# Another written order of 48 interleaved strands, with 13 unread products in place of 52

## The chip, the cores and the metric

The kernel runs on one core of one Trainium2 chip. The metric is device time in microseconds (us) of one execution; the figure of a version is the median of its runs.

## What is computed

The reference is two layers over x of shape (4, 512, 128), float32. Each layer normalises x, runs an attention s and a mixture of experts g on the result, and adds their gated product:

```python
xn = _layernorm(x)
s = _L0_attn_ref(xn, ...)            # three branches: compressed, selected, window of 32
g = _silu(_L0_ffn_ref(xn, ...))      # 8 experts, 2 of them per token
x = x + s * g
xn = _layernorm(x)
s = _L1_attn_ref(xn, ...)            # full attention, 16 heads of 8, plus residual
g = _silu(_L1_ffn_ref(xn, ...))      # one of 8 experts per token is kept
x = x + s * g
```

An expert is a 128 to 512 to 128 network with relu. Layer 1's batches are the 4 batches of 512 tokens again; its attention takes all 512 keys of a batch.

## The kernel before, in words

The work is cut into 48 generators, called strands. Each `yield` ends a step: a handful of instructions, mostly on one engine. Nothing in the program decides at run time which strand goes next. A string, `ORDER`, names the strand of every step, and `advance` walks through it and issues the step's instructions. The five engines (PE is TensorE, DVE VectorE, ACT ScalarE, POOL GpSimd, SP the queue of most transfers) each get their instructions in that order, and the framework adds the semaphore waits and leaves the order alone (`manual_schedule`). So the string sets the order of every queue.

```python
        self.advance(dict(zip(string.digits + string.ascii_letters, strands)))
...
        for s in "".join(ORDER.split()):
            if s == ".":
                self.busy()
            else:
                next(strands[s], None)
```

A `.` calls `busy` (L1247): one 128x128 product of the identity with itself into a part of a PSUM tile that nobody reads. It leaves two matmul records in the trace.

The characters stand for these strands, in the order of the list in `both`; in the text a letter with a number is the n-th step of a strand:

- 0 to 3: layer 0's norm, transpose, router and gate logits of one batch each; 4 to 7: `enter`, the end of layer 0 and the start of layer 1 for one batch. Its steps: 1 loads the picked expert rows (`yg`, on SP), 2 to 4 weigh and add them (POOL, DVE, DVE), 5 tanh on ACT, 6 silu, gate with `s` and add x (DVE), 7 to 10 layer norm (DVE, POOL, DVE, POOL; step 10 is six POOL instructions), 11 and 12 transpose and copy, 13 and 14 router logits, 15 to 18 queries (product, split into high and low parts, four writes to DRAM, one strip read of 1 MB), 19 to 22 the same for keys, 23 and 24 values.
- 8, 9: small set-up of layer 0 and of layer 1 (`lnb`). a, b: routing of batches 0, 1 and of 2, 3 (`route`, with `dispatch`): step 2 the rank product, 3 to 5 DVE, 6 the product that inverts the list, 7 the lists of rows and experts.
- c to f: values of layer 0's attention per batch; g to j: keys and queries; k to n: the attention itself (steps 1 and 4 window scores, 7 compressed scores, 10 selected scores, 13, 14, 16, 17 the weighted sums `o` of one tile each, 15 and 18 their normalisation on DVE, 19 to 22 transpose, copy, output projection, addition).
- o, p, q, r: layer 0's experts in 46 tiles of 128 rows. o loads a tile's weights (578 KB, SP), p fetches its rows (indirect, POOL), q transposes four tiles' rows, then per tile the hidden product `hid` (L367) and relu to `h` (ACT), r the output product `y` (L394), the bias addition on DVE (L403) and the scattered store to `ys` (POOL, L406). Weight buffers: four; `hid` and layer 0's `y` have one PSUM buffer each, so a y product needs the addition of the one before it.
- s: buffers of layer 1's values. t, u: layer 1's scores, top-2 and the scaled rows `xw` stored to `xs` (t of batches 0, 1; steps 5 and 7 are the stores). v: layer 1's routing over all tokens.
- w, x: layer 1's attention in 64 units: w the scores `st` (L1079) and two exponentials of 1021 ns on ACT, x the weighted sum `av` (L1100). y, z, A, B: turning and projecting its result per batch.
- C, D, E, F: layer 1's experts, 23 tiles, like o, p, q, r but with relu on DVE. G: silu of layer 1's expert rows, step 1 loads them. H to K: last gate and store per batch. L: the certificate.

Some couplings set by the order: strand E needs v's lists, v needs all four batches' router logits, and so `enter` of batches 2 and 3, which needs all of r and the attention of batch 3 (n22). The scores of unit after unit reuse two PSUM pairs that ACT must have read. The k strip of a batch (step 22 of `enter`) is loaded into the buffer that held attention probabilities of layer 0.

Of the kernel before, what the change touches and what calls it, by code (L numbers as in the profile page):

```python
# [62 lines left out]


ORDER = """
v800010....00.c1201c2c31102319283139c12a2323a2a8.gaa8.........aaaoapoaa8aopgo.............3pg3bp
pp.....bggpb..qpqpqqrpbqpqrboqrqgrprbbbqorqr8bcqrbgcorrcgcpbrqb...cgorgpkcppkqkggg...kqrkrkqgork
qrkrqkorqkrkrqqkorrrqpgoqdgrdhdphhphhqpqhrrqdqrrrqoqrroqqrqphoqqhrqrdprdqdorrdqdprhhpqokrdqrrkor
rkkrqqorrrqpkoqrqkpqrpqqrphhkhoqkrqrqqqrpqkhohrrkhpriorriipreipoeireiiiliiqe.iiill......lqrilirl
orijeejjeleelelljflfjlfljjjlfjjq.jjllqrjlffqfffrlqorrlrfjjorlljlmqm4qqrp5qrqmpoqmrprmprqmorqm44r  # L70
m45qmr5or4m54qrmqrq4orr5qm4pqmr4or5qpqr5pqqrpmorrm4mr4oq4qmr555rmqqqq4qrq4orrrqpqomrrmpqqrmpom4r
r4pq4rqrrqosq5rn5orrnp4rqnppppppppoq5rr5ttrqtqorrqq4qqqtqnttttr4ror4nrqnrrqonrorrnqnrqnorrnqnq5r
ooooorr5q5rqrrqqnrrqqr5rqqqrrrnrrnnnss4675n455..w66wn46w776.w7wx6w6w7wx6w6665n6wwx6w6ww6w6xw6xw5
wx5wwxwyynwnwx7ww7wxwx777ww7x7w7w7wxuwyywuuwxwwwxwvwxwvxwywwxwwv66wwvx6wwx6uwxwuuwxyuuvvwyCwywxC
ywyCywCDwx6D6w6wDwxDwx7Dw7wx7DwyDwyzwEDzwxDwEwEEDwxDwwEEDwxwxwFzwFECzFExwwxwFwFECwFEwExDEwxDwwxD
FzFwCDzwEEFwxwwxwFwFECwFE7wxwwxwx7z7wwx7zzzwzFzFCFzwwEEwxwwxw77w7wxwxFwFACwFAEwEEExDwxDwwDFwFECD
wEwxFwwxwxFwFACwFAEwExwwxwFwFECwFEwxwwxwxFEFECFEEAwDAwxDwFEDDDDDDDDFECwFwxwFwFECwFEwxwwxwxFEFECF
AwALwxwFEwEwExEAwFACFwAwxwAAwwxwxFEFECFwwxwFEFECFwwxwFwFECwFEwxwwxwxBFBwFwECEFEwxEwwxwBBFEFECCCC
CFwwxwFEFEFwwxwxFEFEEFwwxwBFBwFwxFwFwFwxFFwwxxxBGBLLBBLBBGBGGHHHGGGGGIIIJJJKKK
"""  # L80


# [2227 lines left out]
```

## Time and profile before

| | before |
|---|---|
| median of 3 runs | 508.03 us (505.74 to 514.65) |
| profiled execution | 502.39 us |
| its span, first to last instruction | 500.6 us |
| mean granted TensorE clock | 0.939 |
| matmuls | 4355 records, busy 432.1 us |

The times of steps and waits come from the profiled execution, so a sum of them is compared with its 502.39 us and 500.6 us. The page gives busy time per engine, the chain that ended last and the costliest groups of instructions; the trace answers for stretches of time, waits and single instructions. In its rows a bracket at the end says how long the engine stood idle before the instruction and what it waited for. DMA-issuing rows (SPq, POOLq) are issues: the data lands later.

### The profile page before, as it was taken

The page shows a single profiled execution, that of the slowest core. Times are in us where ns is not written, and L with a number is a line of the kernel's source. Part 1 is how long each engine was busy: PE and PEld are TensorE (multiplying, and loading weights), DVE is VectorE, ACT ScalarE, POOL GpSimd, SP SyncE. Part 2 cuts the span into 40 slices and gives each one's busy share as a digit, 9 for nine tenths or more (in the row PEclk, how much of TensorE's full clock was granted, in tenths as well). Part 3 has the DMA queues.
Part 4 walks back from the last instruction along what each step waited for, and adds up shares of the span by engine and source line. Part 5 has one row for each costly group of instructions (what it writes and reads, how often), then busy time and mean ns, then how long its engine had stood idle before and what let it go on. Part 6 is the DMA issues. An engine that isn't in the chain of part 4 may idle for free.

```text
span 500.6 us, 11299 instructions
## 1 busy us (share of the span) xinstructions
PE 432.1 (86%) x4355; PEld 307.7 (61%) x4355; DVE 270.6 (54%) x819; ACT 246.2 (49%) x417; POOL 176.8 (35%) x194
## 2 busy tenths in 40 slices
PE   5977799798999898989598969789899999999950
PEld 5765687787768787978477723224454556656620
DVE  5797754156767728444432666695235434643445
ACT  1101773543384375234262157667567676667530
POOL 2136535534500166976032250404441144121300
PEclk9997999999999899979799579999899999999985
DMA  8834546955665366359975632039547744544233
GB/s 269 199 107 145 164 130 205 248 174 175 202 138 108 106 197 185 119 173 255 316 227 181 206 132 85 0 122 313 198 125 229 231 134 119 163 125 139 64 97 89
DMA packets 50302, 82.49 MB, mean 165 GB/s; under 512 B 5520, under 2 KB 30240, under 8 KB 50240
## 3 DMA queue, kind: packets, MB, share of 16 engines
q1 hardware_dynamic: 45248, 71.30, 46.9%
q0 software_dynamic: 4416, 9.05, 7.2%
q10 hardware_dynamic: 576, 1.34, 0.7%
q8 instruction: 36, 0.59, 0.5%
q14 instruction: 26, 0.21, 0.1%
HBM read 64.56 MB, written 17.11 MB: 163 GB/s over the span
## 4 chain that ended last, share of the span: by engine, by line
PE 44%; DVE 14%; DMA 6%; issue 4%; POOL 4%; ACT 2%; SPq 0%; ACTq 0%; POOLq 0%; DVEq 0%
PE av L1100 10%; PE y L394 8%; PE hid L367 6%; PE st L1079 4%; DMA wt<-in_w 2%; PE o L838 2%; PE sw L761 2%; PE otr L1118 1%; DMA xr<-xs,d_where 1%; PE so L891 1%; PE o L830 1%; POOL xr L344 1%; DVE yg L437 1%; ACT h L379 1%; DVE yg L432 1%
## 5 line engine op out<-in xcount | busy, mean ns | idle before, releaser
L1088 ACT ACTIVATE p<-st 128x1024 f32<-128x1024 f32 x128 | 124.2, 1021 | 75.3 <-PE st L1079 75.2
L406 POOL DMA_INDIRECT ys<-y,d_where x69 | 69.3, 1005 | 181.4 <-DVE y L403 123.9
L344 POOL DMA_INDIRECT xr<-xs,d_where x69 | 67.5, 978 | 78.6 <-DMA xs<-xw 24.4
L394 PEld LDWEIGHTS y<-wt,h 128*128 128x128 f32 x552 | 70.8, 196 | 36.8 <-ACT h L379 15.8
L394 PE MATMUL y<-wt,h 128*128 128x128 f32 x552 | 81.9, 293 | 10.7 <-ACT h L379 6.3
L367 PE MATMUL hid<-xts,wt 128*128 128x128 f32 x552 | 79.9, 290 | 10.5 <-DMA wt<-in_w 6.4
L379 ACT ACTIVATE h<-hid,wt 128x128 f32<-128x128 f32 x184 | 52.4, 369 | 73.2 <-issue 40.7
L367 PEld LDWEIGHTS hid<-xts,wt 128*128 128x128 f32 x552 | 70.9, 201 | 17.6 <-issue 7.2
L1100 PE MATMUL av<-p,va 128*32 128x512 f32 x512 | 70.0, 619 | 1.3 <-ACT p L1088 1.1
L403 DVE TENSOR_TENSOR y<-y,wt 128x128 f32<-128x128 f32 x69 | 19.9, 289 | 93.0 <-PE y L394 73.2
L1079 PE MATMUL st<-stq,stk 32*128 32x512 f32 x256 | 40.7, 507 | 5.2 <-ACT p L1088 5.1
L381 DVE TENSOR_SCALAR h<-hid,wt 128x128 f32<-128x128 f32 x92 | 25.9, 343 | 24.9 <-PE hid L367 24.9
L1079 PEld LDWEIGHTS st<-stq,stk 32*128 32x128 f32 x256 | 16.6, 186 | 36.0 <-ACT p L1088 27.1
L770 ACT ACTIVATE pw<-sw 128x1024 f32<-128x1024 f32 x16 | 15.6, 1021 | 14.0 <-PE sw L761 14.0
L1100 PEld LDWEIGHTS av<-p,va 128*32 128x32 f32 x512 | 10.2, 108 | 16.8 <-issue 12.4
L1110 DVE COPY oT<-av 128x512 f32<-128x512 f32 x16 | 11.0, 688 | 15.1 <-PE av L1100 15.1
L362 ACT COPY xts<-xt 128x512 f32<-128x512 f32 (+2 forms) x18 | 10.3, 572 | 17.6 <-PE xt L359 17.6
L838 PE MATMUL o<-v,pc 128*128 128x36 f32 x128 | 18.4, 292 | 0.0
L838 PEld LDWEIGHTS o<-v,pc 128*128 128x128 f32 x128 | 16.5, 201 | 0.8
L761 PEld LDWEIGHTS sw<-qT,kw 32*128 32x128 f32 x512 | 16.4, 194 | 0.5 <-issue 0.3
L761 PE MATMUL sw<-qT,kw 32*128 32x64 f32 x512 | 16.3, 275 | 0.0
L359 PE MATMUL xt<-c_ident,xr 128*128 128x128 f32 x69 | 12.1, 287 | 4.4 <-DMA xr<-xs,d_where 4.0
(254 smaller groups left out, 597.5 us busy)
## 6 DMA issues: line engine op xcount, KB each, us to landing
wt<-in_w SPq DMA_DIRECT2D x69, 578.0 KB, 4.0
v<-drv SPq DMA_DIRECT2D x16, 256.0 KB, 6.2
drq<-hl SPq DMA_DIRECT2D x16, 256.0 KB, 3.3
stq<-drq SPq DMA_DIRECT2D x4, 1024.0 KB, 5.2
drk<-hl SPq DMA_DIRECT2D x16, 256.0 KB, 3.0
stk<-drk SPq DMA_DIRECT2D x4, 1024.0 KB
yg<-ys SPq DMA_DIRECT2D x12, 256.0 KB, 3.1
xr<-xs,d_where POOLq DMA_INDIRECT x69, 4.4
```

Source lines behind the costliest of these rows:

```text
L344: nc.gpsimd.indirect_dma_start(out=rows[i // 4][:, i % 4, :], out_offset=None, in_=self.xs[ks[i // NS]], in_offset=bass.IndirectOffsetOnAx ...
L367: nc.tensor.matmul(ps[:, f, :], wt[:, W_1 + f * P : W_1 + (f + 1) * P], xt[:, i % 4 * P : (i % 4 + 1) * P], start=True, stop=True,)
L379: nc.scalar.activation(h[:, f, :], ps[:, f, :], AF.Relu, bias=b1)
L381: nc.vector.tensor_scalar(h[:, f, :], ps[:, f, :], b1, 0.0, ALU.add, ALU.max)
L394: nc.tensor.matmul(ps[:, 0:D], g["h"][:, f, :], g["w"][:, W_2 + f * D : W_2 + (f + 1) * D], start=(f == 0), stop=(f == NF - 1),)
L403: nc.vector.tensor_tensor(y, ps[:, 0:D], g["w"][:, W_B2 : W_B2 + D], ALU.add)
L406: nc.gpsimd.indirect_dma_start(out=views[i], out_offset=bass.IndirectOffsetOnAxis(ap=to[:, i % NS : i % NS + 1], axis=0), in_=y, in_offset ...
L761: nc.tensor.matmul(ps[g // 2][:, g % 2, jj * 2 * QB : (jj + 1) * 2 * QB], a["kw"][g32(g), j].rearrange("p h r -> p (h r)"), qT[g32(g), j * ...
L838: nc.tensor.matmul(out(0, g, 4), pc[g // 2][:, g % 2, t * P : (t + 1) * P], flat(a["vc"][:, g]), start=True, stop=True,)
L1079: nc.tensor.matmul(ps[hp][:, i, :], ks[r, t, k * P : (k + 1) * P], qs[r, t, :], start=True, stop=True,)
L1088: nc.scalar.activation(e, ps[hp], AF.Exp, scale=SCALE)
L1100: nc.tensor.matmul(av[32 * h : 32 * h + 32, :], va[:, k, (4 * t + h) * 32 : (4 * t + h) * 32 + 32], e[h // 2][:, h % 2, :], start=(k == 0) ...
```

## The change

Only the string `ORDER` is replaced. It has 1287 steps in place of 1326, because it has 13 dots in place of 52. All other strands have as many steps as before, in their own order, so the instructions of the computation, their shapes and their buffers are the same; what changes is how the strands lie against each other on all five queues.

- The dots between the routing of batches 0, 1 and the first experts (positions 48 to 109) go from 30 to 7; those further on go from 17 to 1. The first five stay.
- Set-up strand 8 ends at step 34 of the string, not at 140. Values and keys of batch 0 (c, g) and its attention (k) come earlier: c ends at 88 (was 169), k starts at 121 (was 168).
- Attention of batch 3 (n) ends at 685, just after the first scores of layer 1 (w1 at 679); before, it ended at 779, after w22 (w1 at 720).
- The loads of `enter` 2 and 3 (6, 7) come after the first units of layer 1's attention; `u` and `v` (scores and routing of layer 1) lie closer together, the stores u5 and u7 now ahead of v2. Layer 1's experts start at 849 (was 901).
- At the end the load G1 stands before the last scores' sums (x78), not behind them, and the gates of batches 0 and 1 (H1, I1) before the last addition of s (B13), not behind it.

```diff
--- before.py
+++ after.py
@@ -63,20 +63,20 @@
 
 
 ORDER = """
-v800010....00.c1201c2c31102319283139c12a2323a2a8.gaa8.........aaaoapoaa8aopgo.............3pg3bp
-pp.....bggpb..qpqpqqrpbqpqrboqrqgrprbbbqorqr8bcqrbgcorrcgcpbrqb...cgorgpkcppkqkggg...kqrkrkqgork
-qrkrqkorqkrkrqqkorrrqpgoqdgrdhdphhphhqpqhrrqdqrrrqoqrroqqrqphoqqhrqrdprdqdorrdqdprhhpqokrdqrrkor
-rkkrqqorrrqpkoqrqkpqrpqqrphhkhoqkrqrqqqrpqkhohrrkhpriorriipreipoeireiiiliiqe.iiill......lqrilirl
-orijeejjeleelelljflfjlfljjjlfjjq.jjllqrjlffqfffrlqorrlrfjjorlljlmqm4qqrp5qrqmpoqmrprmprqmorqm44r
-m45qmr5or4m54qrmqrq4orr5qm4pqmr4or5qpqr5pqqrpmorrm4mr4oq4qmr555rmqqqq4qrq4orrrqpqomrrmpqqrmpom4r
-r4pq4rqrrqosq5rn5orrnp4rqnppppppppoq5rr5ttrqtqorrqq4qqqtqnttttr4ror4nrqnrrqonrorrnqnrqnorrnqnq5r
-ooooorr5q5rqrrqqnrrqqr5rqqqrrrnrrnnnss4675n455..w66wn46w776.w7wx6w6w7wx6w6665n6wwx6w6ww6w6xw6xw5
-wx5wwxwyynwnwx7ww7wxwx777ww7x7w7w7wxuwyywuuwxwwwxwvwxwvxwywwxwwv66wwvx6wwx6uwxwuuwxyuuvvwyCwywxC
-ywyCywCDwx6D6w6wDwxDwx7Dw7wx7DwyDwyzwEDzwxDwEwEEDwxDwwEEDwxwxwFzwFECzFExwwxwFwFECwFEwExDEwxDwwxD
-FzFwCDzwEEFwxwwxwFwFECwFE7wxwwxwx7z7wwx7zzzwzFzFCFzwwEEwxwwxw77w7wxwxFwFACwFAEwEEExDwxDwwDFwFECD
-wEwxFwwxwxFwFACwFAEwExwwxwFwFECwFEwxwwxwxFEFECFEEAwDAwxDwFEDDDDDDDDFECwFwxwFwFECwFEwxwwxwxFEFECF
-AwALwxwFEwEwExEAwFACFwAwxwAAwwxwxFEFECFwwxwFEFECFwwxwFwFECwFEwxwwxwxBFBwFwECEFEwxEwwxwBBFEFECCCC
-CFwwxwFEFEFwwxwxFEFEEFwwxwBFBwFwxFwFwFwxFFwwxxxBGBLLBBLBBGBGGHHHGGGGGIIIJJJKKK
+8v00010....00.c1210c2c812102381188833c21a92329a23a3gcc3ccaag3.....aaagoaopacgaopoabpgppgc.bpgbp.
+qqpqqprbpqqrpgoqqrbrgqprokrqrkqrkobbpkqbrbgprkqkprbogqgrkgbrpkqkqrggorrgbdrorkddhkqhqkrkrordqqrh
+rorkhqkhqpdqdpdkdhpqprdrorqdqrqroqrrqroqrrqhqproqhrqrhhpqpkroqrrkpqqhkrhoqhrkqrqkqpqqprhohrrkhep
+roiereripirorliielqiliqriqrqorriilroreqeeiieeiqrlqlp.lqrpeoiqlrilpfqiprffjrorljjlqjqrfljrolrjjlj
+jjqllqrjjqrjoqrrqlqpffprfoqlfr4fq5prpjjqrqfojrrqr44oqlr4rl455q4qqlqpr4oqrqr54l5pmr4or5rm44rm5oqq
+m4qmrrm5p54qrm5o44mqm44mqqmrrqmmprorrp4mroprqmqrpqqprmorrqrqorrqrqorrqmqprorqmqsrqqpppppppprmoqr
+mqrqrqorrqrmqorrmnrorqn5n45qn44rnqrnor5qr5ttntqnnnq5nqtqrqttrroooooqnnttr5r5rnrrqnqrn5rrnss4qnqq
+rnr5rrnw5nw5wn4w4wx6w7wxwwwxw5w566w57xw67w76xw67ywxw6wxw76w66w6w7xw6wyxw777w6x76w76w7w66x7uwuxwu
+wywxwwwuxwyuwvuxuuwvxwwywxwwywvxw6w6vv6w6xwvwCwxDwCxwCDywCyDxywwyDyw6D6w7wD6x7Dw7EwDxwDyxEwyDEwE
+wFDEFDECxFwFwwEFECFFEEEFxEDCwEFwEwFDEFEDCxFwFwDwEFECFxwxFwwEFECFExEDwxwDwzDFzwFDECwEFwxwxwwzxFzw
+FECwFEwxwxwwzFzwFECwFE7w7x7w7xwwFxwFCEwFEwExDEwxDwwzDDDDDDDD77zzw7xwwzFzwFECwFEwxwxzwxwzAwAxwwFw
+FCEwFEwxwxwwFxwFCAwFxAwEEwxwwFwFCxwFwEEwxwwExFEwFACwFxAwEEwxwwFwFCxwFwEEwxwwFxwFCAwFxAwLEwxwwFAw
+EAwxFACwFEEwxwwExAEwABwxBwFwFCCCCCxwFwEEwxwwFwFxwFwExEwBwxBwFwFxwFwEEEwxwwFwFxwFwFxwFBwFFxBwwxww
+wGxwwwxxxBGBLGGLHBBHHBGLGBIGIIBJGGJJKKK
 """
 
 
```

## The prediction

> A strand's letter with a number is its n-th step (r136: step 136 of strand r); times are us from the start of the span.
>
> **What bounds the kernel now.** First the page's busy shares, then busy time by stage, cut at four places that I found by laying the written order over the trace's matmuls: first expert product of layer 0 (q3, 43.8), last one (r136, 269.6), first expert product of layer 1 (E3, 356.4), last attention product (x79, 478.6).
>
> ```profile
> PE 432.1 (86%) x4355; PEld 307.7 (61%) x4355; DVE 270.6 (54%) x819; ACT 246.2 (49%) x417; POOL 176.8 (35%) x194
> 0.00:43.80 43.80, 31.60 (x168) 26.58 (x168) 33.62 (x157) 5.22 (x9) 13.45 (x23) 1.00 0.69 199
> 43.80:269.60 225.80, 201.06 (x2575) 171.81 (x2575) 118.18 (x336) 109.00 (x264) 101.79 (x107) 0.95 0.62 179
> 269.60:356.40 86.80, 73.97 (x639) 36.27 (x639) 53.80 (x147) 47.53 (x54) 26.55 (x30) 0.89 0.49 161
> 356.40:478.60 122.20, 120.81 (x953) 70.09 (x949) 53.35 (x157) 81.90 (x87) 35.04 (x37) 1.00 0.46 140
> 478.60:500.60 22.00, 4.68 (x26) 3.00 (x26) 11.65 (x23) 2.49 (x4) 0.00 (x0) 0.62 0.35 100
> ```
>
> Columns: length, PE, PEld, DVE, ACT, POOL, granted clock, DMA. TensorE's written order is the spine, but only the fourth stage is solid (120.8 of 122.2). The first hangs on VectorE (33.6 of 43.8, from 6 us on nearly solid), the third on a chain through all engines, the last on VectorE and the stores.
>
> Busy time flatters PE, so I count steps instead: the start-to-start time of a step that waits for nothing. Expert product (hid or y) 0.99, av 1.00, st 0.44, window scores 2.06, an o step of attention 0 2.10, wide projection 0.95, otr 0.49, an unread product 0.22. All steps of the program give 369.7, the 52 unread products 11.6; the rest of the span is waiting or half clock. By stage, work without unread products: 13.7, 181.0, 56.5, 115.8, 3.3. (The third, say: 22 av 22.0, 24 st 10.6, three o 6.3, five otr 2.5, the first y 1.0, seven projections for keys, queries and values 7.0, eleven other steps of 0.3 to 1.0 together 7.1.) The timeline then shows what the waiting is:
>
> ```profile
> 211.71 1.16 PE L367 MATMUL hid<-xts,wt 128*128 128x128 f32 x8 [0.52 <-ACT xts L362]
> 215.14 2.08 PE L394 MATMUL y<-wt,h 128*128 128x128 f32 x8 [2.27 <-DVE y L403]
> ...
> 243.72 2.04 PE L367 MATMUL hid<-xts,wt 128*128 128x128 f32 x8 [5.04 <-DMA wt<-in_w]
> ...
> 210.51 1.11 DVE L136 TENSOR_SCALAR zn<-x,mv_z,rs_z 128x128 f32<-128x128 f32 x4 [4.74 <-POOL rs_z L141]
> ...
> 278.24 0.38 SPq L1039 DMA_DIRECT2D stk<-drk  x1
> 278.93 3.06 SPq L419 DMA_DIRECT2D yg<-ys  x4
> ...
> 307.41 1.06 PE L891 MATMUL so<-c_wa,aoT 128*128 128x128 f32 x8
> ...
> 343.30 1.10 POOL L344 DMA_INDIRECT xr<-xs,d_where  x1 [24.36 <-DMA xs<-xw]
> ...
> 353.64 0.33 PE L359 MATMUL xt<-c_ident,xr 128*128 128x128 f32 x1 [1.17 <-DMA xr<-xs,d_where]
> ```
>
> The reader is to see: a y product late because VectorE stood 4.74 us at zn (its scale was behind 5 us of POOL work in 410); one weight load late by 5.04; layer 0's results (yg) loaded only after SP was let past the k strip; attention 0's last projection (n21) at 307.4, which enter3 needs; layer 1's fetch waiting for the stores xs; and E1 waiting for the fetch.
>
> **What the Trainium skill says.** "TensorE: Matmul & The Clock Gate", What's actually happening: the array runs at half clock after about one idle window of 3.4 us. This trace agrees: the clock records between front and tail have half-rate stretches of 3.4, 6.8 or 10.2, and the product after the 2.27 wait took 2.08. The same page, Architectural detail: other engines' queues are strict FIFO; the 4.74 at zn with the y addition behind it agrees. "DMA: Bandwidth & Descriptors", Anatomy of one DMA: a DMA's wait is on the issuing sequencer, so what is behind it waits too; the pair at 278.24 agrees. "Perfetto Trace Analysis", Identifying the Most-Contended Engine: matmul busy share is no measure of headroom; hence my count.
>
> **The change, stage by stage.** No instruction of the computation changes, so each duration above holds; only the order does, on all five queues, and 39 of 52 unread products go.
>
> Front, 43.8. The 23 products that go here stood in PE waits, so they are worth nothing. VectorE's path to the fetch list (a7): setup1's 0.84 moves behind a1, one wait of about 1 us on the lnb matmuls goes, and 0.15+0.23+0.68+0.19 of small steps come ahead: even. From a7 to the slot that q1 needs (middle of b3) VectorE has 7.1 against 7.3. Cover that goes: without products PE may be at half clock in b2 and g7, 0.5. I take 44.3 (43 to 46.5). By then one projection and one cv (1.95) more are done.
>
> Layer 0, 225.8 = 181.0 work + 44.8 waits, cold clock and unread products. After: three o steps come in from the next stage (+6.3), a projection and a cv are done already (-1.95): 185.4. The 44.8:
> - The y addition that stands behind zn on VectorE: the next y product now comes 6.6 us of PE work after its own (r88 to r91), not 4.4 (r91 to r94), which covers a zn wait like the 4.74. The excess of three steps at 211 to 219 (gaps 3.43, 1.87, 1.71 for 0.99 each) goes, -4.
> - Layer 1's first q strips (two transfers of 1 MB) move away from close-packed weight loads: the late one had 5.9 us of PE work ahead of its product; the loads behind the strips now have 7.0 to 8.0. The gap was 6.07 for a step of 0.93, and the cold steps after it cost 2.2: of 7.3 I take -5.
> - l4 has six product steps ahead of it in place of seven unread ones and a 0.6 wait: -2.3. Attention 0's first scores go between the first expert tiles, -1.5.
> - Against: 17 tiles instead of 12 have y straight behind hid, each 0.58 for ACT's h (the gap of 1.57 at hid 83.9): +3. Enter0 and enter1 now put 21 us of VectorE work beside 16 of PE: the y additions queue, I work out 2.1 at r76 and about 1 later: +3. A y addition behind the routing step t4 (5 us on DVE): +1.2.
> That leaves 39.2, and 224.6.
>
> Chain to layer 1, 86.8 for 56.5 of work. Work falls by three o (6.3), two st and two av (2.9), one otr (0.5): 46.8. The chain sets the end, so its links count, from r136: y, addition, POOL issue, landing 1.0+0.3+1.0+2.3, then SP: 521's four writes (2.5) and the yg load: 6 (was 9.4: the k strip 422 now goes before r136). Landing 6 (was 6.7): 12. POOL 1.0, VectorE adds, silu, layer norms of both batches in one run to enter3's tr_z: 28 (was 44.8, because n21 came at 307.4; it now follows w1). Logits, scores, top-2, routing on VectorE: 24.5 more, was 25.7. The stores u5, u7 now precede the routing, so the fetch starts at once (3.2 before). Fetch to transposes 10.7 and on to E3 2.4, as before (343.3 to 356.4 is 13.1): 65.7. A chain of some dozen hand-overs isn't that tight; I give each 0.4: 70.7 (64 to 80).
>
> Layer 1, 122.2. Two st, two av and an otr more: 119.2; the old waits 6.4; tiles 0 to 2 have 0, 1.4 and 0 us of PE work between hid and y, where before it was 3.8 or more, and h takes VectorE 1.4 (4 of 343 ns): +2.5. 128.1 (125 to 136).
>
> Tail, 22.0. Behind the last addition of s VectorE has 12 passes of 0.69 now, and will have 5: the first two gates move into PE's last steps. Not all of 4.8 is kept, since those seven passes now delay B11 and B13: by hand 13.4 from x79's end to the last pass, was 15.1. The yg load can come then, the last y product being 5.8 us of PE work ahead of x79 and not 2.5. 20.3 (19 to 23).
>
> Sum: 44.3+224.6+70.7+128.1+20.3 = 488.0, against the span's 500.6: -12.6. On the profiled execution's own 502.4 that is 489.8. The runs shown have their median 508.0, 5.6 above it; the same 12.6 off it gives **495.4, taken as 495**.
>
> **Rivals.** (A) No gain to be told: the waits move. The chain is shorter on paper, but its DVE passes share the queue with oT copies and y2, y4, y6, and enter0/enter1's crowd costs 8 in place of 3. Stage three 76, layer 0 231: sum 499.7, or 507. For it: VectorE has 22 us beside 16 of PE work there, was 18; against: most waits of before stand in one place each, and the new order takes just those apart.
> (B) Larger gain: the chain does run at 65.7 and the weight stall goes whole (7.3): 480.7, or 488.
> (C) Slower: weights of layer 1's tiles 4 to 7. Their loads are issued 5.8 to 7.2 us of PE work ahead (before: 9.6 to 16), while 717 and 622 move 2 MB. The load that was late at 243.7 took about 11 us. If all four take that, 4 x 5 = 20, and half clock over the 14 or so us of steps between, +7: beyond 6 us a load it decides, and 495+27 = 522. Against it: the median landing of wt is 4.0.
> (D) The products that go kept the clock up: 43.4 to 50.3 was cold with them; if another two windows (6.8) of real work run at half rate, +3.4: part of the range.
>
> **Chances.** Forecast 0.50 (487 to 503), A 0.27, B 0.15, C 0.08. Unknown costs are about 6 each way in layer 0 and 8 in the chain, and three-run medians differ by 1%; a range of 482 to 511 leaves 0.2 out. About 2% is what this measurement can tell from no change: below 497.9 is faster, and the forecast lies 2.5 us under it. Of the forecast 0.45 falls under it: with B faster 0.60, same 0.31, and with C slower 0.09.
>
> **What would show it.** Right: E3 some 16 us nearer r136's start; n21 before the yg load is read; no wait over 3 us for wt in layer 0; a zn wait that no y product shows; unread products 26 records instead of 104; five VectorE passes behind the last s. Wrong: the y additions of r77 to r86 late by more than 5 in all; E13 to E19 waiting for wt; v7 more than 55 us behind r136; granted clock below 0.92.

## The result, and the profile after

The new order takes 488.11 us (median of 4 runs, 485.76 to 492.38) against 507.0 for before beside it (4 runs, 505.74 to 514.65): a ratio of 0.9645, with a 95% interval of 0.9554 to 0.9735. The forecast was 495, range 482 to 511. The profiled execution took 485.76, its span 483.9 (forecast 489.8 and 488.0).

Executions of one program differ by 3% on one chip (before: 494 to 510 in 31 runs) and by nearly 5% on another (535 to 561 in 51), so the runs below are given as medians of all runs with their number. A ratio with its 95% interval compares only the fast runs of both kernels, which favours the kernel that ran more often, so the two can differ.

The busy line of the page:

```profile
PE 418.2 (86%) x4277; PEld 292.9 (61%) x4277; DVE 267.6 (55%) x819; ACT 245.7 (51%) x417; POOL 179.5 (37%) x194
```

Busy time by stage, cut at the same four steps as before (q3, r136, E3, x79). The columns behind the stretch are length, PE, PEld, DVE, ACT, POOL, granted clock, DMA share, GB/s:

```profile
0.00:44.80 44.80, 32.62 (x134) 25.79 (x134) 33.85 (x155) 7.67 (x13) 15.12 (x29) 0.92 0.65 195
44.80:263.60 218.80, 196.00 (x2765) 168.12 (x2765) 121.34 (x349) 106.20 (x260) 103.82 (x103) 0.98 0.65 189
263.60:334.80 71.20, 58.80 (x377) 24.75 (x377) 46.73 (x134) 43.67 (x50) 25.29 (x27) 0.95 0.52 166
334.80:463.60 128.80, 125.83 (x981) 71.17 (x977) 54.10 (x160) 85.91 (x92) 35.23 (x37) 1.00 0.48 149
463.60:483.90 20.30, 4.91 (x26) 3.07 (x26) 11.56 (x23) 2.25 (x4) 0.00 (x0) 0.61 0.22 63
```

The busy share of PE is 86% as before, though the program is 16.7 shorter: it tells nothing. Set against the steps' work (the sum of what each step takes when it waits for nothing), the stages read as follows; "waits" is the stage less that work, so half clock and unread products are in it.

| stage | before | forecast | after | waits before | waits after |
|---|---|---|---|---|---|
| front | 43.8 | 44.3 | 44.8 | 30.1 | 29.2 |
| layer 0 | 225.8 | 224.6 | 218.8 | 44.8 | 33.4 |
| chain to layer 1 | 86.8 | 70.7 | 71.2 | 30.3 | 24.4 |
| layer 1 | 122.2 | 128.1 | 128.8 | 6.4 | 9.6 |
| tail | 22.0 | 20.3 | 20.3 | 18.7 | 17.0 |

Four of the five are within 0.7 of the forecast, and layer 0 is 5.8 better. The timeline lines that answer to those of before (start, duration, engine and line, what; in brackets the idle time before and its releaser):

```profile
190.87 1.29 DVE L136 TENSOR_SCALAR zn<-x,mv_z,rs_z 128x128 f32<-128x128 f32 x4 [5.07 <-POOL rs_z L141]
...
198.38 1.09 POOL L406 DMA_INDIRECT ys<-y,d_where  x1 [0.18 <-issue]
...
203.00 0.29 DVE L403 TENSOR_TENSOR y<-y,wt 128x128 f32<-128x128 f32 x1 [7.62 <-issue]
...
203.44 2.05 PE L394 MATMUL y<-wt,h 128*128 128x128 f32 x8 [3.33 <-DVE y L403]
...
269.12 1.33 PE L891 MATMUL so<-c_wa,aoT 128*128 128x128 f32 x8
...
270.45 2.49 SPq L419 DMA_DIRECT2D yg<-ys  x4
...
321.23 1.10 POOL L344 DMA_INDIRECT xr<-xs,d_where  x1 [21.13 <-DVE d_where L316]
```

VectorE still waits 5.07 at zn, and no y product near it shows that. But a y product is late by 3.33 at 203.4, and it and the step behind it ran at half clock: the addition that it needs was held for 7.62. The row names no cause ("issue"). By the trace's landing records it is the store in front of it: r90, issued at 198.38, landed at 202.92, and the addition, which writes the same one of two y buffers, started at 203.00. No product waits for wt in layer 0 any more. n21 (L891) now comes before the yg load and not 28 behind it; layer 1's fetch is released by the list (d_where), no longer by the stores of xs. Of these stores only u5 stands ahead of v2 in the new order (places 779 and 781); u7, at 784, is ahead of v3, and both were issued some 10 before v7 began (307.4, 308.5, 318.8).

### The profile page after: what moved, and what is told of

The parts are those of the page before. It is cut to its first block, busy times and chain, and to the rows that moved or that the text cites. A ratio compares the mean times of both kernels' runs of the same rounds, so it can differ in the third digit from the quotient of the medians.

```text
span 483.9 us, 11137 instructions
## 1 busy us (share of the span) xinstructions
PE 418.2 (86%) x4277; PEld 292.9 (61%) x4277; DVE 267.6 (55%) x819; ACT 245.7 (51%) x417; POOL 179.5 (37%) x194
## 4 chain that ended last, share of the span: by engine, by line
PE 33%; DVE 9%; issue 3%; DMA 3%; ACT 2%; POOL 1%; DVEq 0%; ACTq 0%
PE av L1100 10%; PE y L394 6%; PE hid L367 6%; PE st L1079 5%; ACT p L1088 2%; DMA stk<-drk 2%; PE so L891 2%; DMA xr<-xs,d_where 1%; PE otr L1118 1%; PE v L1044 1%; DVE yg L437 1%; PE sw L761 1%; DVE yg L432 1%; PE xt L359 1%; POOL xr L344 1%
## 5 line engine op out<-in xcount | busy, mean ns | idle before, releaser
L344 POOL DMA_INDIRECT xr<-xs,d_where x69 | 69.1, 1001 | 80.5 <-DVE d_where L316 21.1
L394 PE MATMUL y<-wt,h 128*128 128x128 f32 x552 | 80.8, 290 | 14.7 <-ACT h L379 8.4
L394 PEld LDWEIGHTS y<-wt,h 128*128 128x128 f32 x552 | 70.1, 192 | 32.0 <-ACT h L379 13.1
L367 PE MATMUL hid<-xts,wt 128*128 128x128 f32 x552 | 77.5, 284 | 4.3 <-ACT h L379 2.9
L367 PEld LDWEIGHTS hid<-xts,wt 128*128 128x128 f32 x552 | 68.1, 193 | 21.0 <-issue 10.4
L362 ACT COPY xts<-xt 128x512 f32<-128x512 f32 (+2 forms) x18 | 10.3, 574 | 21.3 <-PE xt L359 21.1
L838 PE MATMUL o<-v,pc 128*128 128x36 f32 x128 | 17.4, 283 | 0.0
L761 PEld LDWEIGHTS sw<-qT,kw 32*128 32x128 f32 x512 | 15.6, 187 | 1.4 <-ACT kw L628 1.2
L838 PEld LDWEIGHTS o<-v,pc 128*128 128x128 f32 x128 | 15.6, 192 | 1.0 <-issue 0.3
L830 PEld LDWEIGHTS o<-v,pw 128*32 128x32 f32 x992 | 11.3, 113 | 4.5 <-issue 3.3
```

Of the source, the lines that this page charges most:

```text
L344: nc.gpsimd.indirect_dma_start(out=rows[i // 4][:, i % 4, :], out_offset=None, in_=self.xs[ks[i // NS]], in_offset=bass.IndirectOffsetOnAx ...
L367: nc.tensor.matmul(ps[:, f, :], wt[:, W_1 + f * P : W_1 + (f + 1) * P], xt[:, i % 4 * P : (i % 4 + 1) * P], start=True, stop=True,)
L394: nc.tensor.matmul(ps[:, 0:D], g["h"][:, f, :], g["w"][:, W_2 + f * D : W_2 + (f + 1) * D], start=(f == 0), stop=(f == NF - 1),)
L761: nc.tensor.matmul(ps[g // 2][:, g % 2, jj * 2 * QB : (jj + 1) * 2 * QB], a["kw"][g32(g), j].rearrange("p h r -> p (h r)"), qT[g32(g), j * ...
L838: nc.tensor.matmul(out(0, g, 4), pc[g // 2][:, g % 2, t * P : (t + 1) * P], flat(a["vc"][:, g]), start=True, stop=True,)
```

## The experiments

Twelve kernels ran, four at a time, on three chips. The new kernel itself ran on the third of these only, so on the first two a kernel is compared with the new one by their profiles, across chips. The stages of the profiles (us; the first column is front and layer 0 together), the profiled execution, and the median of all runs; where these two lie apart, the stages are not those of a typical execution:

| kernel | to r136 | chain | layer 1 | tail | span | profiled | median |
|---|---|---|---|---|---|---|---|
| before | 269.6 | 86.8 | 122.2 | 22.0 | 500.6 | 502.39 | 507.0 |
| new | 263.6 | 71.2 | 128.8 | 20.3 | 483.9 | 485.76 | 488.11 |
| dots_out | 276.0 | 87.8 | 122.9 | 21.5 | 508.3 | 510.07 | 509.04 |
| p2_layer0 | 268.1 | 85.1 | 123.0 | 21.0 | 497.3 | 499.04 | 495.88 |
| p3_chain | 263.5 | 78.1 | 121.5 | 22.4 | 485.5 | 487.31 | 490.86 |
| r2_rest | 269.8 | 85.3 | 128.8 | 20.3 | 504.3 | 506.08 | 504.76 |
| fix_store | 263.9 | 72.5 | 128.8 | 20.3 | 485.5 | 487.40 | 490.33 |
| fix_va | 265.1 | 70.0 | 128.8 | 21.3 | 485.3 | 487.06 | 487.12 |
| b_strip | 267.0 | 93.7 | 123.4 | 21.1 | 505.2 | 507.07 | 501.24 |
| dots_in | 264.9 | 77.3 | 129.1 | 20.7 | 491.9 | 493.74 | 492.73 |
| after_again | 314.0 | 72.3 | 136.8 | 21.5 | 544.5 | 546.30 | 544.11 |
| best2 | 314.1 | 76.2 | 132.6 | 21.4 | 544.4 | 546.15 | 546.32 |
| fix_store2 | 308.5 | 72.5 | 136.9 | 21.7 | 539.6 | 541.38 | 544.29 |
| p2_n | 311.9 | 84.0 | 129.2 | 21.4 | 546.5 | 548.36 | 553.13 |

### The unread products alone: dots_out

```diff
 (the order of before)
-23 dots between the routing of batches 0, 1 and q1
-16 of the 17 dots behind q7
```

> The written order of before with 39 of its 52 unread products taken out (23 of the 30 ahead of the first experts, 16 of the 17 later ones) and nothing else changed. My theory (they stand where PE waits anyway, and what is gained by their 0.22 each is lost again to waiting): span 500.6 as before, within 1.5; first expert product of layer 0 still at 43.8, within 1. Rival, the clock: without them further windows of 3.4 of real work run at half rate, +3.4 or more, and the granted clock falls below 0.93. Rival, they cost PE time: 39 x 0.22 = 8.6 less, span 492.

Measured: 509.04 (4 runs) against 503.8 (31 runs), ratio 1.0165 (1.0067 to 1.0264). The windows rows of the first 63 to 66 us behind q3, before first, dots_out second:

```profile
43.80:107.00 63.20, 55.89 (x611) 47.25 (x611) 29.23 (x83) 36.03 (x89) 32.28 (x36) 0.95 0.63 175
```

```profile
43.60:110.00 66.40, 58.22 (x602) 49.59 (x602) 30.21 (x87) 36.19 (x89) 32.67 (x36) 0.90 0.62 170
```

The front came out as expected (43.6): taking 23 products out of it saved nothing. The clock rival holds: in these windows half clock for 3.4 from 45.6 and 10.2 from 62.7 where before had 6.8 from 43.4; then 20.5 in the chain from 288.0; and in all, ahead of the tail, 68 where before has 44 (24 more at half the speed are 12 of full-speed work, part of it in waits anyway). The third theory, that the products cost TensorE time, falls: the kernel became slower. So does mine, for the old order. The products were not free to take away; they were worth 5.2 by the medians, 1%.

### The two halves of the change: p2_layer0, r2_rest, p3_chain

```diff
 p2_layer0:  new order up to r136 | what is left, in the order of before
 r2_rest:    order of before up to r136 | what is left, in the new order
 p3_chain:   new order up to E3   | what is left, in the order of before
```

> The new order up to and with the last y product of layer 0 (r136), and then all steps that are left in the order of before. So front and layer 0 are new, but attention 0's projection n21 still comes 17 us of PE work behind r136 and the stores u5, u7 and all of layer 1 stand as before. My theory, from the waits by stage of the two profiles (front -0.9, layer 0 -11.4, chain -6.0, layer 1 +3.2, tail -1.7): r136 at 263.6 as in the new kernel; chain 73 (n21 some 24 behind r136, and the 49 from n21 to E3 that before has), layer 1 122, tail 22: span about 481, some 4% under before. Rival (the chain's new order is what pays, and layer 0's share is lost again behind it since the three o steps no longer fill the chain's waits): chain 86 as before and the span 494.

> The order of before up to and with r136, and then all steps that are left in the new order: front and layer 0 old, chain, layer 1 and tail new; the steps n14 to n17 of attention 0 that the new kernel has done by then come first in the chain. My theory: r136 at 269.6 as in before; the chain is the new kernel's 71.2 plus some 7 for the three o steps ahead of the yg load = 78, layer 1 128.8, tail 20.3: span 497, within 2% of before. Rival (the early projection and the early yg load make the whole gain): chain 71, span 490.

> The new order up to the first expert product of layer 1 (E3), and then all steps that are left in the order of before. My theory: E3 at 334.8 as in the new kernel; layer 1 then 122.2 plus the 3.4 of scores and sums that are left over = 125.6, tail 22.0: span 482.4, so within 2 of the new kernel (483.9). If layer 1's tiles with y straight behind hid cost nothing, it ends at 484 or above.

Measured on the same chip, where before's median is 503.8: p2_layer0 495.88 (12 runs), ratio 0.9848 (0.9803 to 0.9892); r2_rest 504.76 (20 runs), 1.0078 (1.0018 to 1.0138); p3_chain 490.86 (4 runs), 0.9799 (0.9658 to 0.9940). So by the medians the new front and layer 0 are worth 7.9 alone, all that comes behind them alone nothing, and the new order up to E3 12.9. The links of the chain, behind r136:

| | before | new | p2_layer0 | r2_rest | p3_chain |
|---|---|---|---|---|---|
| n21 | 37.8 | 5.5 | 34.0 | 17.1 | 6.0 |
| batch 3's transpose 711 | 44.8 | 31.9 | 41.0 | 43.7 | 32.7 |
| v7 ends | 70.6 | 57.4 | 67.8 | 69.1 | 58.1 |
| fetch issued (D1) | 73.7 | 57.6 | 70.9 | 69.4 | 58.4 |
| E3 | 86.8 | 71.2 | 85.1 | 85.3 | 78.1 |

Between before and new, 12.9 of the 15.6 are won ahead of 711; from there to E3 it is 42.0 and 39.3 (39.3 to 45.4 in the five). Both of my expectations for the halves were too low. p2_layer0 came out at its rival (chain 86, span 494): chain 85.1, and a span of 494.0 in the median run. In r2_rest the three o steps stood ahead of the yg load and ran at half clock (13.7 of it from 276.4); the last expert's addition r137, behind n18 on VectorE, came 14.0 behind r136 (1.8 in the new kernel), and the first additions of `enter` came 13 later than there, not 7. In the profile of p2_layer0, which is its slowest run of 12, n21 came at 34 and not 24; the attention units ahead of it ran at half clock for 23.9:

```profile
274.60:298.50 23.90, 18.62 (x69) 6.61 (x70) 11.23 (x28) 10.81 (x13) 8.04 (x9) 0.50 0.44 142
```

PE was busy for 18.6 of the 23.9 and its longest wait there was 2.65. In p3_chain E3 did not come at 334.8, as expected, but at 341.6: its fetch is as early as in the new kernel, but by the old order of what was left E3 stands behind 3.4 more of scores and sums, with half clock for 3.4 from 334.2 on top. Work that stands ahead of E3 is missing behind it, so the spans tell the rest: 485.5 against 483.9, 1.6 in favour of the new order behind E3.

### n21 alone: p2_n

```diff
-r136 r137 r138 r139 61 71 ... w1 ... n19 ... n20 ... n21 ... n22
+r136 n19 r137 r138 n20 r139 61 71 ... n21 w1 n22
```

> The mixed order p2_layer0 (new up to r136, old behind it) with one thing more: the last four steps of attention 0, n19 to n22, come directly behind r136 and ahead of w1 as in the new order, not after w8 to w22. In p2_layer0 n21 came 34.0 behind r136, batch 3's transpose 41.0, E3 85.1; in the new kernel 5.5, 31.9 and 71.2. If n21's place holds the chain: n21 at 6, the transpose at 30 to 33, E3 at 74 to 77, span 488. Rival (old order's other steps, the loads 61 and 71 or the later stores u5, u7, hold it): E3 at 82 or more, span 494.

Measured: 553.13 (4 runs) on the third chip, where before has 547.55 (51 runs), ratio 1.0274 (1.0102 to 1.0447): not faster. p2_layer0 did not run on this chip, so the two are compared by their links behind r136. In the profile of p2_n r136 starts at 311.9:

```profile
316.80 1.16 PE L891 MATMUL so<-c_wa,aoT 128*128 128x128 f32 x8 [0.66 <-DVE hl L1028]
...
345.52 0.26 DVE L1124 RECIPROCAL cert<-otr 128x16 f32<-128x16 f32 x1 [2.41 <-PE otr L1118]
...
346.02 0.68 DVE L432 SCALAR_TENSOR_TENSOR yg<-th_a,yg 128x512 f32<-128x512 f32 x1
...
351.61 0.55 PE L161 MATMUL tr_z<-c_ident,zn 128*128 128x128 f32 x3
```

n21 comes at 4.9, and still the silu of batch 3, which alone needed it, runs at 34.1 and the transpose at 39.7: step 76 kept its written place on VectorE, behind the steps of an attention group. E3 comes at 84.0 (85.1 in p2_layer0): the rival holds, and n21's place alone is worth about 1. The other 12.8 of the way to the new kernel's 71.2 come from further steps that the new order moves. Two parts can be read off: the transpose at 31.9 in place of 39.7, and the fetch 0.2 behind v7's end in place of 2.9, since the stores of xs come earlier. Which of the moved steps the transpose needs was not tried one by one.

### A wait in layer 0: fix_store, fix_store2

```diff
 fix_store:
-510 o34 ... m11 r90
+o34 ... m11 r90 510
 fix_store2:
-510 ... r93 ... p40 ... p41 ... p42 r96 ... r97 p43 q85 q86 p44 ... r99 ... r102
+r93 510 ... r96 p40 ... r97 p41 ... q86 p42 ... r99 p43 ... r102 p44
```

> The new order with one step moved: 510, six POOL instructions (6.0 in the new profile, 192.2 to 198.2), now comes behind r90, the scattered store of tile 29, and not ahead of it. In the new profile y product r97 waits 3.33 at 203.4 behind the addition of tile 31, which VectorE holds 7.62 for nothing that the profile names; r90 is issued at 198.4, and the two buffers of the y tile let tile 31's addition start only when that store has left. If that is the cause: no wait over 1 at r97, r136 5 earlier (258.5), span 479. Rival (the addition waits for something else, POOL's backlog of fetches for instance): the wait stays, span 483.9.

Measured: 490.33 (4 runs, 485.17 to 494.47) against 506.95 for before (23 runs) on the second chip. The stretch in fix_store's timeline:

```profile
193.69 1.00 POOL L406 DMA_INDIRECT ys<-y,d_where  x1 [0.33 <-DVE sc L453]
...
201.37 1.00 POOL L406 DMA_INDIRECT ys<-y,d_where  x1 [0.30 <-issue]
...
208.46 0.29 DVE L403 TENSOR_TENSOR y<-y,wt 128x128 f32<-128x128 f32 x1 [4.72 <-DMA wt<-in_w]
...
208.89 2.05 PE L394 MATMUL y<-wt,h 128*128 128x128 f32 x8 [2.47 <-DVE y L403]
```

The wait at r97 went (0.51 is left), so its place was read rightly: the second y buffer, held by a store that POOL had behind 510. But r136 came at 263.9 and not at 258.5. The next store, r93, now stood behind 510 and went out at 201.37, and the addition of tile 32, which uses its buffer, came 7.1 behind that. Its row names a weight load, but by the semaphore records that load landed only at 210.53, after the addition; the last part of r93 landed at 208.38, just ahead of it. r100 waits 2.47, and by q87 the kernel is where the new one is (210.7 in both). The wait gave place to the next in the row.

> The new order with only the layer-0 mend of best2: 510 behind r93, p40 behind r96, p41 to p44 one behind each of r97, q86, r99 and r102. With 510 behind r90 alone the 3.3 wait at r97 went, but the next store r93 came at 201.4 behind 510 and a fetch, and the addition of tile 32 waited for it until 208.5 (PE 2.5). Now r93 goes at 196.5 and r96 at about 203, with tiles 32 and 33 added at 203 and 207. If the stores' place on POOL is the whole cause: no wait over 1 from r94 to r103, r136 at 259 to 260, span 479 to 480. Rival (the wait goes to a later addition once more, or to the fetches that now come late): r136 at 263, span 483.

Measured: 544.29 (20 runs) on the third chip, where the new kernel takes 544.11 (22 runs). TensorE's waits from r94 to r103 are 0.5 at most, but the step m16 between them takes some 7 longer than its 2.1, a loss of this chip (below; at m14 in after_again) that gives the stores time, so this change could not be judged.

### A wait in the chain: fix_va

```diff
-522 w12 523 62 63 w13 524 72 x4 w14 64 73 w15 74 65 x5 w16 66 75 ... w22 611 w23 77 x8 w24 612 w25 y2
+522 62 63 72 64 73 74 w12 65 75 66 w13 x4 w14 w15 x5 w16 ... 611 w22 w23 77 x8 523 w24 612 w25 524 y2
```

> The new order with a few steps of the chain moved: in the new profile VectorE stands 4.82 at the value addition of batch 1 (step 524, 280.2) for its product on PE, with both additions of enter2 and enter3 behind it although their inputs were there at 276.6 to 278.2. Here 523 and 524 come behind x8 and w25, the additions 64, 73, 74 and the tanh and silu steps 65, 75, 66 come ahead of x5, and 611 ahead of w22. If VectorE's order there is on the path to E3: silu of batch 2 some 3.5 earlier (280), its transpose 611 at 287, batch 3's 711 at 292 in place of 295.5, and E3 2 to 3.5 earlier behind r136 (68 to 69 in place of 71.2), span 481. Rival (the units of attention, paced by ScalarE's exponentials, set E3): E3 stays at 71 behind r136.

The new kernel, then fix_va:

```profile
275.56 1.04 POOL L935 TENSOR_TENSOR yg<-yg,rw 128x512 f32<-128x512 f32 x1 [8.62 <-DMA yg<-ys]
...
277.18 1.04 POOL L935 TENSOR_TENSOR yg<-yg,rw 128x512 f32<-128x512 f32 x1 [0.58 <-DMA yg<-ys]
...
280.22 0.69 DVE L1054 TENSOR_TENSOR va<-v,bv 128x512 f32<-128x512 f32 x1 [4.82 <-PE v L1044]
280.82 0.68 DVE L939 TENSOR_TENSOR yg<-yg,yg 128x512 f32<-128x512 f32 x1
```

```profile
278.35 0.69 DVE L939 TENSOR_TENSOR yg<-yg,yg 128x512 f32<-128x512 f32 x1 [1.28 <-POOL yg L935]
...
282.60 1.15 ACT L430 ACTIVATE th_a<-yg 128x512 f32<-128x512 f32 x2
...
283.26 0.69 DVE L432 SCALAR_TENSOR_TENSOR yg<-th_a,yg 128x512 f32<-128x512 f32 x1 [1.98 <-ACT th_a L430]
```

Measured: 487.12 (4 runs) against 506.95 (23 runs), ratio 0.9749 (0.9574 to 0.9925). The addition came at 13.2 behind r136 and not 17.2, but the tanh stood behind an exponential (w12) on ScalarE, and silu came only 1.7 earlier. E3 is at 70.0 and not 71.2: between the two theories. The unchanged chain gave 71.2 to 72.5 in four profiles (new, fix_store, after_again, fix_store2), so VectorE's order was on the path by 1 to 2, if at all, with ScalarE close behind.

### The strip: b_strip

```diff
-... p45 418 r107 q93 ... o41 ... q99 q100
+... p45 r107 q93 ... o41 ... q99 418 q100
```

> The order of before with one step moved: 418, the 1 MB read of batch 0's layer-1 q strip, comes behind q99 on SP and not two weight loads ahead of it. The prediction put the late weight load of q99 (5.04 of waiting, and the cold products after it, 7.3 in all) down to that strip, and 5 of it as what is to be won. If so: no wait for wt above 2 at q99, r136 at 264 in place of 269.6, span 495. Rival (the weight buffer, or the four writes of batch 1's queries, set that load): the wait stays at 5, span 500.6.

```profile
240.54 1.33 PE L367 MATMUL hid<-xts,wt 128*128 128x128 f32 x8 [2.78 <-DMA wt<-in_w]
```

Measured: 501.24 (20 runs) against 506.95 (23 runs), ratio 0.9965 (0.9912 to 1.0018): 5.7 less by the medians, but the ratio's interval takes in 1. The wait for wt goes from 5.04 to 2.78, between the two theories, so the strip makes about half of it; r136 comes 2.6 earlier, at 267.0 and not 264. The profile is of the slowest of the 20 runs, and in it the chain gave that back, with half clock for 10.2, 13.7 and 6.8 in it.

### Products put back: dots_in

```diff
 (the new order)
+16 dots before b2, 4 before q3, 12 before w1, 7 before w4
```

> The new order with 39 unread products more, so 52 as before: 16 ahead of b2 (PE waits 3.9 there), 4 ahead of q3, 12 ahead of w1, 7 ahead of w4. Taking 39 out of the old order cost it some 5 to 8, in windows of half clock that came in their place. If the new order lost the same by it: span 478 or less, granted clock above 0.97. If its waits are now too short to need them: within 1.5 of 483.9; and if they lie in the way of real work there, up to 39 x 0.22 = 8.6 more.

Measured: 492.73 (4 runs) against 506.95 (23 runs), ratio 0.9836 (0.9666 to 1.0006). Beside it on this chip, orders close to the new one took 487.12 (fix_va) and 490.33 (fix_store). The span is 491.9, 8.0 above the new kernel's: the last of the three theories, that the products lie in the way, fits the number (up to 8.6 more), though part of the loss is half clock. The front gained 0.9, layer 0 lost 2.1 and the chain 6.1: w4 came 1.3 later behind r136, and a stretch at half clock came all the same, later on (17.1 from 291.2). So the new order did not want its products back, at these places at least.

### The new kernel on another chip: after_again, best2

```diff
 best2 = fix_store2 and, in the chain:
-522 w12 523 62 63 w13 524 72 x4 w14 64 73 w15 74 65 x5 w16 66 75 ... 67
+522 62 63 72 64 65 w11 73 66 74 75 w12 w13 x4 w14 67 w15 x5 w16 ...
```

> The new kernel unchanged, as the standard for the runs beside it, and as a second profile: how far do its stages repeat. 44.8, 218.8, 71.2, 128.8, 20.3 were measured; front, layer 1 and tail within 0.5, layer 0 and the chain within 4, since two kernels with the same order up to r136 differed by 4.8 there and all by half-clock windows of 3.4 that fell elsewhere.

> The new order with both mends in a second form. In layer 0: 510 behind r93 (not only r90), and the fetches p40 to p44 no longer in a row ahead of the stores but one behind each of the next stores. In the chain: the additions 64, 73, 74 at once when their inputs are there, tanh of batch 2 ahead of the exponentials w11 (in fix_va it stood 1.3 behind one), silu 66 directly behind it and 67 ahead of x5, the value product 523 and its addition behind x8 and w25, 611 ahead of w22. If the two waits are on the path: r136 3 to 5 earlier, E3 3 behind the 71.2 and so 68 behind r136, span 477. Rival (as with the first mends each wait only gives place to the next one): within 2 of the new kernel, 482 to 486.

Measured: the new kernel 544.11 (22 runs), best2 546.32 (14 runs), before 547.55 (51 runs); ratios 1.0096 (1.0036 to 1.0156) and 1.0031 (0.9945 to 1.0116). On this chip the gain is gone: 3.4 by the medians, 0.6%, and none by the ratio. best2 is no better than the new kernel; its tanh and silu came 4 earlier, but the layer norm step 69 waited behind 76 on VectorE, the units of attention slipped 5, and E3 came at 76.2.

Front, chain and tail repeat within 1.2; layer 0 takes 50 more. Layer 1 takes 8 more, which was not followed up. What an sw step looks like in the timeline of the new kernel's first profile; then layer 0's row and the same step on this chip:

```profile
58.78 2.10 PE L761 MATMUL sw<-qT,kw 32*128 32x64 f32 x64
```

```profile
44.80:314.00 269.20, 232.02 (x2765) 197.35 (x2765) 121.93 (x350) 105.88 (x260) 102.93 (x103) 0.87 0.53 154
```

```profile
62.07 1.33 PE L761 MATMUL sw<-qT,kw 32*128 32x64 f32 x34
63.84 0.35 PE L761 MATMUL sw<-qT,kw 32*128 32x64 f32 x3 [0.43 <-issue]
...
66.02 0.72 PE L761 MATMUL sw<-qT,kw 32*128 32x64 f32 x5 [0.26 <-issue]
```

The 64 products run through in 2.1 there; here they start well and then come three to five in 0.7, with gaps that nothing in the profile releases ("issue"). Over the 24 steps of this kind the loss against an unhindered step is 38.9, where the first profile has 3.9: 35 of the 50. It falls on the same few steps in all four kernels of this chip. What holds them there was not tested, and before has no profile on this chip, so why before loses less there (41 by the medians, the new order 56) stays open.

## Why the prediction was right, step by step

- **Chain (70.7, measured 71.2).** The links, measured and in brackets forecast: yg load read at 6.9 (6), first addition at 11.1 (12), transpose at 31.9 (28), v7 25.5 behind it (24.5), fetch at once (0.2), E3 13.6 behind that (13.1). The 5 for hand-overs came out in its sum (5.5), but partly by luck: it was set as 0.4 at each of a dozen, and 3.9 had gone by the transpose, where VectorE stood 4.82 at the value addition, though taking that wait out gave 1 to 2 at most (fix_va). p2_layer0, r2_rest and p2_n show that no single one of the moves tried gives this gain. The line drawn for v7 (wrong if more than 55 behind r136) was too tight: it started at 55.2 and ended at 57.4, and with the 5 of hand-overs the forecast's own v7 lies at 57.5.
- **Layer 0 (224.6, measured 218.8).** The work was right; the waits fell by 11.4 and not 5.6. Term by term, forecast and then measured from the trace: late weight load and cold after it -5, -7.3 (all of it; in b_strip the strip alone gives about half of the wait); first tiles and scores between them -1.5, -0.3; dots and the wait at l4 -2.3, and measured -4.2 for the dots alone; close y products +3, +2.1 (17 waits of y for h in place of 13, 8.4 in all in place of 6.3); y behind t4 +1.2, +1.6. Mis-sized: the enter0/enter1 crowd, +3, where TensorE's waits from 150 to 199 are 1.4 in all (4.2 in before between the same times) and no y addition is late. Not foreseen: half clock at l19 (3.6 before, 0 after).
- **The step that failed** in layer 0 is the -4 for the y product behind zn. That product is indeed free, though zn still waits (its scale, step 58, stands behind 410 and a store on POOL). But the next batch's six POOL instructions, 510 (192.2 to 198.2), stood ahead of the scattered store r90, the store held one of the two y buffers, and q83 to m16 lost 5.7 where 4.9 had been lost around the old jam: +0.8 in place of -4. The prediction looked at who waits on VectorE and not at what waits behind 510 on POOL. The terms measured add up to -10.9 of the -11.4.
- **Layer 1 (128.1, 128.8) and tail (20.3, 20.3).** Layer 1's waits rose by 3.2 (2.5 forecast, for the tiles with y close behind hid); of that the profile shows 1.2 as waits for h and 0.6 for attention's exponentials, so the forecast's reason covers less than half. No load of tiles 4 to 7 was late, so rival C's transfer never came. Behind the last addition of s there are five VectorE passes, as written down:

```profile
474.01 0.68 DVE L896 TENSOR_TENSOR s<-so,res 128x512 f32<-128x512 f32 x1
474.62 0.68 DVE L437 SCALAR_TENSOR_TENSOR yg<-yg,s 128x512 f32<-128x512 f32 x1
475.33 0.69 DVE L438 TENSOR_TENSOR o<-yg,x 128x512 f32<-128x512 f32 x1
475.94 0.69 DVE L432 SCALAR_TENSOR_TENSOR yg<-th_b,yg 128x512 f32<-128x512 f32 x1
476.66 0.69 DVE L437 SCALAR_TENSOR_TENSOR yg<-yg,s 128x512 f32<-128x512 f32 x1
477.39 0.69 DVE L438 TENSOR_TENSOR o<-yg,x 128x512 f32<-128x512 f32 x1
```

- **Products and clock.** "Worth nothing" held in the new order, where the clock rose from 0.939 to 0.962 with 39 products fewer; that the waits which they had covered are shorter there is a likely reason, not a tested one. In the old order it would have been wrong by 5 to 8 (dots_out). Rival D named the mechanism, on the wrong order.
- **Clock or waits.** The forecast has only small terms for the clock. Half-clock stretches ahead of the tail come to 44 in before's profile and to 20 in the new one's; 24 less of them are up to 12 of full-speed work, part of it in waits anyway. A second estimate: over the 31 runs of before on one chip, a granted clock higher by 0.01 goes with a time shorter by 2.2 (a fitted line, correlation -0.61), which for the 0.023 between the two profiles gives 5 of the 16.7. Waits and half clock go together, and no run parts them, so how much of the gain is the clock's stays open.
- **Between A and B.** With a gain of 18.9 by the medians and 16.7 by the spans, the result lies at rival B's 488; but B's reason, a chain at 65.7, was not met: the chain took the forecast 71. Of the 7.3 between 495.4 and 488.11, layer 0 brought 5.8 and the other stages took 1.7 back; the other 3.2 come from the medians, which lie 5.6 above the profiled execution in before and 2.4 in the new kernel. A's crowd (8) and its chain of 76 did not come.

## What to carry to other kernels

In a fixed order, cost a stage as work plus waits, and follow each wait to the queue that causes it: what stands behind that step on its own queue, stores and buffers too, is the next wait when this one is covered. A step moved forward gains little while the steps that use its result keep their written places (p2_n), and half of a reordering can be worth nothing alone (r2_rest). Filler work on TensorE is judged by the clock records of the kernel without it, and a gain of a few per cent is only known for the chips it was measured on.

## What the runs showed of the hardware

- TensorE stayed at half clock for 23.9 while busy for 18.6 of it, with no wait over 2.65 (p2_layer0). The Trainium skill, "TensorE: Matmul & The Clock Gate", What's actually happening, has the clock back after about 3.4 us of sustained work. This trace does not agree: the last wait in the stretch ended at 286.86, and half clock lasted to 298.5, through 11.6 of steps without a gap (as the profile models their ends); the scores (st) still take 0.80 there, and 0.51 at 303.07. In dots_in it is 16.5 without a gap (291.8 to 308.3). Nor does half clock need an idle stretch of 3.4: in before it began at 214.1, where TensorE's longest wait was the 2.27 of the prediction's lines. What starts and ends such a stretch was not found.

```profile
286.86 1.25 PE L161 MATMUL tr_z<-c_ident,zn 128*128 128x128 f32 x4 [2.65 <-DVE zn L136]
...
297.03 0.80 PE L1079 MATMUL st<-stq,stk 32*128 32x512 f32 x4
```

- One chip ran the same program 11% slower (544.11 against 488.11), mostly in dense rows of tiny products (35 of the 50 more in layer 0) that came three to five in 0.7 with gaps that nothing in the profile released.
- The addition that reuses a store's buffer started 7.1 after the issue of that store (201.37 to 208.46 in fix_store), 4.6 in the new kernel (198.38 to 203.00), where the median landing of such a store is 4.2. With two buffers a store that is issued late, or lands late, holds the addition after next; why the one in fix_store landed late was not tested.
